# Where a whole group's outputs are scaled and where GpSimd's sums are called, in a mixture-of-experts tail on one core

## The chip, the core and the metric

The kernel runs on one core of a Trainium2 chip, in fp32. The metric is the device time of one execution in microseconds (us), given as the median of several runs. The profile is of one execution with the hardware profiler. Five engines run side by side, each with its own list of instructions in order: TensorE (PE, with its weight loads PEld), VectorE (DVE), ScalarE (ACT), GpSimd (POOL) and SyncE (SP, which here only issues DMAs). They wait for one another by semaphores.

## What is computed

One layer: a graph step (`adj @ h`), then a transformer block whose feed-forward part is a mixture of 8 experts, of which each token uses two. The change lies in the experts alone:

```python
flat = _rmsnorm(x, ln2_w).reshape(-1, Cx)
probs = jax.nn.softmax(flat @ router_w.T, axis=-1)
tp, ti = jax.lax.top_k(probs, TOPK)
tp = tp / (jnp.sum(tp, axis=-1, keepdims=True) + 1e-09)
weights = jnp.sum(tp[..., None] * jax.nn.one_hot(ti, NE, dtype=flat.dtype), axis=1)
out = jnp.zeros_like(flat)
for e in range(NE):
    hh = jax.nn.silu(flat @ w1[e].T) * (flat @ w3[e].T)
    out = out + weights[:, e:e + 1] * (hh @ w2[e].T)
return x + out.reshape(Bx, Tx, Cx)
```

There are 4096 tokens of 256 features; an expert has 682 hidden features.

## The kernel before

The kernel writes each token's row to the lists of its two experts in DRAM, and then works through groups of tokens of one expert: whole groups of 256 tokens (number below `NW`, 25) and small ones of 128 for what is left over. `TURNS` sets the order, and `k` is the place in it, from 0 to 41. Places 0 to 8 are whole groups. From 9 on whole and small groups alternate, except that places 15 and 16, 24 and 25, and 31 and 32 are two small groups in a row; 39, 40 and 41 are whole. So between 9 and 39 a whole group comes either behind one small group (k = 10, 12, 14, 19, 21, 23, 28, 30, 35, 37, 39) or behind two (k = 17, 26, 33).

The main loop (from L1984) does for each k: the hidden layer of group k (`hidden` or `hidden_seven`), then `combine(k - 1)`, the second layer of the group before with the weighting and the output, and then the loads of the weights and tokens of groups k + 4 and k + 5. TensorE so has the work of two groups between each other.

**Hidden layer in seven products.** Whole groups from k = 12 to 39 (`SPLIT13`) use `hidden_seven`: the matrix product in 2x2 blocks with seven block products instead of eight, in two parts, `one` (four chunks of 128 hidden features) and `two` (one chunk). Each part has three PSUM banks: hA, hD and hB. `begun` makes the first product in hA, which ScalarE copies to `s1`, the second in hD, which it copies to `s5`, and the third in hB. `second` adds a product to hA, copied by ScalarE to `u2`, and one to hD. `added_up` adds hB to `s1` and hD to `u2` on VectorE; between these it transposes token rows of coming groups (`turn`). `third` adds once more to hA. All these products are L1609, the copies L1615, the additions L1618. `multiplied` (L1653, L1654) makes the hidden values in SBUF, and `split` (L1704 to L1707) their four block sums on VectorE.

**The block sums of the first weights** are made by GpSimd in `sums13` (L1542 to L1545), four sums of 128x640 values. It is called at the end of an iteration and takes the next group of `SPLIT13` in turn, if that is at most five places ahead and fewer than two are waiting. Before the change it is called whenever `TURNS[k - 1]` is a whole group. Those of the second weights are made by VectorE in `sums2` (L1723 to L1726), right behind the hidden layer of the small group that comes before a whole one.

**combine.** For groups in `SEVEN` (whole, from k = 4 to 39) `seven_products` (L1747) makes seven products in two PSUM banks, ye_y and ye_ms; ScalarE copies one (L1754) and VectorE makes seven additions (L1755 to L1761). A small group has plain products (L1846) in bank ye_y. Both pools have one bank. `gates` makes the tokens' weights on VectorE: `pick` (L1505) and `gt` (L1510). ScalarE scales the output by `gt` (L1857), in two halves for a whole group and one for a small one. For each half GpSimd issues an indirect DMA that adds the rows to DRAM (L1868), behind a memset of `gap` (L1867).

**Order of the loads.** Behind the outputs of an iteration GpSimd sets a cell, `sent` (L2005); SyncE writes that cell to DRAM (L2006) and only then issues the loads that stand behind it in its queue: second weights `load2` (L1403), first weights `load13` (L1397), tokens `load_squares` (L1441) and rows `load_rows` (L1448).

The PSUM banks of the hidden layers are a pool of six (`e_h`), used in turn.

Of the kernel before, what the change touches and what calls it, by code (L numbers as in the profile page):

```python
# [45 lines left out]
NW = -((NE * (GR - 1) - 2 * N) // GR)  # L46
# [5 lines left out]
ALONE = 9  # L52
LAST = 3
RARE = 4
NM = NG - RARE
TURNS = list(range(ALONE)) + [
    g for _, g in sorted(
        ((g - first + 0.5) / (end - first), g)
        for first, end in ((ALONE, NW - LAST), (NW, NM)) for g in range(first, end)
    )  # L60
] + list(range(NW - LAST, NW)) + list(range(NM, NG))
# [5 lines left out]
def fast_kernel(  # L67
# [618 lines left out]
    with (  # L686
# [707 lines left out]
        def load13(k):  # L1394
            i = TURNS[k]
            expert_of[i] = entry(table[0:1, 1, i : i + 1], NE - 1)
            nc.sync.dma_start(  # L1397
                w13s[k % 5], w13[bass.ds(expert_of[i], 1)].rearrange("o p c w -> p (o c) w")
            )

        def load2(k):
            i = TURNS[k]
            nc.sync.dma_start(  # L1403
                w2s[k % 5],
                w2[bass.ds(expert_of.pop(i), 1)].rearrange("o p k c -> p (o k) c"),
            )
# [26 lines left out]
        def load_squares(k):  # L1433
            i = TURNS[k]
            n = halves(i)
            z = squares_room(k)[:, 0 : n * C].rearrange("p (m e) -> p m e", e=2 * Q)
            tokens = lists[bass.ds(place_of(i), n * P), 0:C].rearrange(
                "(m i) (g e) -> g i m e", i=Q, g=4
            )
            for g in range(4):  # L1440
                loaded(i, nc.sync.dma_start(z[g * Q : (g + 1) * Q], tokens[g]))  # L1441
# [45 lines left out]
        def turn(k):  # L1487
            n = halves(TURNS[k])
            turned = squares_room(k + 4)[:, 0 : n * C]
            nc.vector.transpose(turned, squares_room(k)[:, 0 : n * C])  # L1490
            turned_of[k] = turned.rearrange("p (m c i) -> p c m i", c=2, i=Q)
# [9 lines left out]
        def gates(k, r):  # L1501
            i = TURNS[k]
            n = halves(i)
            pick = ex.tile([P, n, NE], F32, tag="pick", name=f"pick_{i}")
            nc.vector.tensor_mul(  # L1505
                pick, r[:, 0:n, 1:KEPT],
                mine[:, i : i + 1, :].to_broadcast([P, n, NE]),
            )
            gt = ex.tile([P, n, 1], F32, tag="gt", name=f"gt_{i}", bufs=3)
            nc.vector.tensor_reduce(gt, pick, AX.X, ALU.add)  # L1510
            return gt
# [55 lines left out]
                )  # L1567
            sums13_of[k].update(m)

        def hidden_seven(k, step, behind):  # L1570

            i = TURNS[k]
            m, xT, w13_sb = sums13_of.pop(k), inputs_of.pop(i), w13s[k % 5]
# [43 lines left out]
            def added(dst, q, bank):  # L1617
                nc.vector.tensor_add(dst, dst, bank[:, 0 : len(q.chunks), :])  # L1618

            def begun(q):  # L1620
                product(q, q.A, "A11", "B11", True)
                copied(q.s1, q, q.A)
                product(q, q.D, "S1", "T1", True)
                copied(q.s5, q, q.D)
                product(q, q.B, "A12", "B21", True)

            def second(q):
                product(q, q.A, "S2", "T2")
                copied(q.u2, q, q.A)
                product(q, q.D, "S4", "B22")  # L1630

            def added_up(q, behind=()):
                behind = iter(behind)
                for j in behind:
                    turn(j)
                    break
                added(q.s1, q, q.B)
                for j in behind:
                    turn(j)
                added(q.u2, q, q.D)  # L1640

            def third(q):
                product(q, q.A, "S3", "T3")
# [13 lines left out]

            sums2(k)
            begun(one)
            second(one)  # L1660
            added_up(one, turns_in.pop(k, []))
            step()
# [155 lines left out]
        def combine(k):  # L1818
            i = TURNS[k]
            n = halves(i)  # L1820
            w2_sb = w2s[k % 5]
            hT = hidden_of.pop(i)
            r = rows.pop(i)
            gt = gates(k, r)
            if k < ALONE or k % 2:
                y = ax.tile([P, HALF, C], F32, tag="yT1", name=f"y_{i}")
            else:
                y = (
                    pt_all[:, 2 * (2 * W13 + W2) :] if k % 4
                    else wo_sb.rearrange("p j o -> p (j o)")[:, 0:512]  # L1830
                ).rearrange("p (h c) -> p h c", h=HALF)

            last = k >= NM - 2
            seven = k in SEVEN
            if seven:
                done = seven_products(k)
            else:
                ps = [
                    pool.tile([P, HALF, C], F32, tag=tag, name=f"ye_{i}_{tag}")
                    for pool, tag in ((p_ms, "ms"), (p_y, "y"))[0 if last else 1 :]  # L1840
                ]

            def products(h):
                cols = slice(h * P, (h + 1) * P)
                for q in range(NF + 1):
                    nc.tensor.matmul(  # L1846
                        ps[h if last else 0][:, h, :],
                        hT[:, q, cols], w2_sb[:, q, :], start=(q == 0), stop=(q == NF),
                    )

            for h in range(0 if last or seven else n):
                products(h)
            for h in range(n):
                if last:
                    products(h)
                if seven or n == 1:
                    nc.scalar.activation(  # L1857
                        y[:, h, :],
                        done[h].rearrange("p h o -> p (h o)") if seven else ps[0][:, h, :],
                        AF.Copy, scale=gt[:, h],  # L1860
                    )
                else:
                    nc.vector.tensor_scalar(
                        y[:, h, :], ps[h if last else 0][:, h, :], gt[:, h], None, op0=ALU.mult
                    )
                at = bass.IndirectOffsetOnAxis(ap=r[:, h, 0:1].bitcast(I32), axis=0)
                nc.gpsimd.memset(gap, 0.0)  # L1867
                put = nc.gpsimd.indirect_dma_start(  # L1868
                    out=(acc_dram if k < NM - LAST else out)[:, :],
                    out_offset=at,  # L1870
                    in_=y[:, h, :], in_offset=None, compute_op=ALU.add,
                )
                if h:
                    free(put, f"half {i}", "an expert has a token once")
                else:
                    join(put, f"half {i}")
                if i < NA:
                    free(put, "last x", "the tokens of the first groups are others")
                    join(put, "first sums")
# [92 lines left out]
        def step():  # L1972
            for f in next(rest, []):
                f()

        sent = ax.tile([1, 1], F32, name="sent", bufs=1)
        sent_dram = tc.dram_tile([1, 1], F32, name="sent_dram")
        load13(2)
# [5 lines left out]
        for k in range(NM):  # L1984
            if k == 3:
                sc_scope.close()
                p_h.append(ctx_h.enter_context(tc.tile_pool(name="e_h", bufs=6, space=PSUM)))
            if k == NM - 1:


                between = iter([lambda: None, lambda: combine(k - 1)])
            if k in SPLIT13:
                hidden_seven(k, step, k + 1)
            else:
                hidden(
                    k, step if k < NM - 1 else lambda: next(between)(),
                    k + 1 if k + 1 < NM else None,
                )
            step()
            if k + 1 in SPLIT13 and TURNS[k] >= NW:  # L2000
                sums2(k + 1)
            if 0 < k < NM - 1:
                combine(k - 1)
                if k + 4 < NM:
                    nc.gpsimd.memset(sent, 0.0)  # L2005
                    nc.sync.dma_start(sent_dram, sent)  # L2006
            if k + 4 < NM:
                load2(k + 4)
            if k + 5 < NM:
                load13(k + 5)  # L2010
            if k + 4 < NM:
                if k + 5 < NM:
                    load_squares(k + 5)
                load_rows(k + 4)
            if 0 < k < NM - 1:
                step()
                if k >= ALONE and TURNS[k - 1] < NW:
                    sums13(k)
            if k == NM - LAST:
                nc.sync.dma_start(out, acc_dram[0:N, :])  # L2020
        combine(NM - 1)
        ctx_h.close()
    kv_scope.close()
    return lists
# [739 lines left out]
```

## Time and profile before

| what | us |
|---|---|
| runs before (three), median | 1534.4 |
| lowest and highest of them | 1533.94, 1540.28 |
| the profiled execution | 1535.82 |
| its span in the profile | 1534.1 |

The span is from the first to the last recorded instruction of the core; the execution's time has 1.7 us around it. The page cuts the span into 40 equal slices, of 38.4 us each; a digit is the busy share of an engine in tenths, and PEclk is the clock that was granted to TensorE:

```profile
PE   9999999999999999999999999999999999998997
DVE  7764665755755677879879878785676767776772
ACT  2102012021021456665665655653222333333331
POOL 2102022121221331374554653452524545536342
PEclk9999999999999999999999999999999999999999
DMA  6344444543544000011011011059778897988765
```

The experts are the last third, from about slice 27. There TensorE is busy nearly all the time, GpSimd about half of it, and the DMA engines at 0.7 to 0.9. An instruction's line in the timeline has its start, its duration, engine and line, what it writes and reads, its shape, how many were merged, and in brackets how long the engine stood idle before it and what ended that.

### The profile page before, as it was taken

To read this page: it belongs to the slowest core of one execution; us is meant where nothing else is said; L and a number is where in the kernel's file an instruction comes from. 1 tells how busy PE (TensorE), PEld (TensorE's weight loads), DVE (VectorE), ACT (ScalarE), POOL (GpSimd) and SP (SyncE) were. 2 spreads that over 40 slices of the span, in tenths; PEclk is the share of its full clock that TensorE was granted. 3 is DMA by queue.
4 is the path that set the end of the run, shared out by engine and by line. 5 is a ranking of instruction groups with operands and counts; after the bars stand their busy time and mean duration, and the time that the engine had idled before them with its cause. 6 is when DMAs were issued, how large, how long until landed. Compare 5 with 4: busy or idle time off the path is not lost. (4 is left out here: it accounts for less than half of the span.)

```text
span 1534.1 us, 28641 instructions
## 1 busy us (share of the span) xinstructions
PE 1509.4 (98%) x10795; PEld 1113.2 (73%) x10795; DVE 1067.1 (70%) x2223; ACT 551.0 (36%) x991; POOL 559.2 (36%) x649
## 2 busy tenths in 40 slices
PE   9999999999999999999999999999999999998997
PEld 8888888888888543444444444358899999998996
DVE  7764665755755677879879878785676767776772
ACT  2102012021021456665665655653222333333331
POOL 2102022121221331374554653452524545536342
PEclk9999999999999999999999999999999999999999
DMA  6344444543544000011011011059778897988765
GB/s 240 131 134 151 156 141 147 167 153 121 178 141 151 4 1 30 15 58 33 26 57 37 29 37 36 22 156 325 211 208 222 261 269 219 269 246 239 225 150 136
DMA packets 105774, 212.19 MB, mean 138 GB/s; under 512 B 62394, under 2 KB 82106, under 8 KB 91994
## 3 DMA queue, kind: packets, MB, share of 16 engines
q1 hardware_dynamic: 92090, 192.00, 38.6%
q0 software_dynamic: 12720, 17.47, 6.3%
q8 instruction: 87, 1.43, 0.4%
q10 hardware_dynamic: 816, 0.79, 0.2%
q14 instruction: 61, 0.50, 0.1%
HBM read 184.48 MB, written 27.13 MB: 138 GB/s over the span
## 5 line engine op out<-in xcount | busy, mean ns | idle before, releaser
L785 PE MATMUL sc<-qT_all,kT 64*64 64x512 f32 (+3 forms) x2304 | 282.1, 557 | 0.5 <-ACT pt_all L793 0.3
L532 PE MATMUL acc<-a,g 128*128 128x256 f32 x1024 | 244.0, 379 | 0.0
L532 PEld LDWEIGHTS acc<-a,g 128*128 128x128 f32 x1024 | 193.5, 190 | 31.8 <-issue 6.7
L785 PEld LDWEIGHTS sc<-qT_all,kT 64*64 64x64 f32 x2304 | 91.2, 133 | 128.6 <-issue 109.2
L793 ACT ACTIVATE pt_all<-sc 128x1024 f32<-128x1024 f32 (+3 forms) x157 | 148.6, 954 | 96.9 <-PE sc L785 93.3
L532 PE MATMUL acc<-more_sums,g 128*128 128x256 f32 x512 | 126.3, 379 | 0.0
L1868 POOL DMA_INDIRECT acc_dram<-y,late x40 | 62.6, 1564 | 172.2 <-ACT y L1857 99.6
L813 DVE TENSOR_TENSOR late<-late,pt_all 128x1024 f32<-128x1024 f32 (+3 forms) x91 | 106.8, 1173 | 24.3 <-POOL pt_all L795 9.9
L433 ACT COPY qT_all<-tr 128x512 f32<-128x512 f32 x30 | 16.2, 588 | 258.7 <-PE tr L431 258.7
L532 PEld LDWEIGHTS acc<-more_sums,g 128*128 128x128 f32 x512 | 97.2, 190 | 13.2
L827 PE MATMUL y_first<-pt_all,vv 64*64 64x512 f32 (+3 forms) x448 | 106.6, 554 | 0.0
L625 POOL TENSOR_TENSOR rot<-rot,tables 128x512 f32<-128x512 f32 x21 | 33.6, 1601 | 198.6 <-ACT rot L621 158.4
L827 PE MATMUL y_second<-pt_all,vv 64*64 64x512 f32 (+3 forms) x436 | 104.2, 555 | 0.0
L1790 PE MATMUL h<-late,qT_all 128*128 128x256 f32 (+1 forms) x616 | 104.0, 327 | 0.1
L1790 PEld LDWEIGHTS h<-late,qT_all 128*128 128x128 f32 x616 | 93.5, 191 | 9.8 <-ACT late L1477 1.0
L1075 POOL DMA_INDIRECT lists<-row,slots x64 | 88.3, 1380 | 17.5 <-issue 15.0
L1797 DVE TENSOR_TENSOR late<-si,h 128x256 f32<-128x256 f32 (+2 forms) x87 | 39.4, 466 | 78.6 <-ACT si L1796 53.3
L827 PE MATMUL y_third<-pt_all,vv 64*64 64x512 f32 (+3 forms) x372 | 88.7, 555 | 0.0
L621 ACT ACTIVATE rot<-pq 32x512 f32<-32x512 f32 x84 | 49.4, 588 | 82.6 <-DVE qT_all L619 43.6
L813 DVE TENSOR_TENSOR sum_all<-sum_all,pt_all 128x1024 f32<-128x1024 f32 (+3 forms) x51 | 56.0, 1098 | 15.8 <-POOL pt_all L795 9.5
L793 ACT ACTIVATE late<-sc 128x1024 f32<-128x1024 f32 (+3 forms) x55 | 50.9, 927 | 41.4 <-PE sc L785 36.7
L532 PE MATMUL acc<-qT_all,g 128*128 128x256 f32 x256 | 65.7, 379 | 0.0
(493 smaller groups left out, 3301.4 us busy)
## 6 DMA issues: line engine op xcount, KB each, us to landing
a<-in_adj_dram SPq DMA_DIRECT2D x64, 1024.0 KB
qT_all<-in_w_dram SPq DMA_DIRECT2D x18, 1408.0 KB
pt_all<-in_w_dram SPq DMA_DIRECT2D x16, 1408.0 KB
res_all<-in_w_dram SPq DMA_DIRECT2D x17, 768.0 KB
pt_all<-in_w_dram SPq DMA_DIRECT2D x16, 768.0 KB
res_all<-in_w_dram SPq DMA_DIRECT2D x8, 1408.0 KB
qT_all<-in_w_dram SPq DMA_DIRECT2D x9, 768.0 KB
late<-lists SPq DMA_DIRECT2D x96, 64.0 KB
```

The lines of the kernel that those rows point to most:

```text
L433: nc.scalar.copy(dst[:, :, cols], tr.rearrange("p c t i -> p c (t i)"))
L532: nc.tensor.matmul(acc[bank][:, at, :], g[jb][:, right, k, :], m[left][:, k, :], start=(jb == 0 and k == 0 and at == 0), stop=(jb == NB - ...
L621: nc.scalar.activation(rot[n * Q : (n + 1) * Q, :], pj[(n ^ 1) * Q : ((n ^ 1) + 1) * Q, :], AF.Copy, scale=1.0 if n % 2 else -1.0,)
L625: nc.gpsimd.tensor_mul(rot, rot, tables[b][:, 1, :])
L785: nc.tensor.matmul(ps[k * HP : (k + 1) * HP, j, :w], kT[sb][hd, i * P + k * HP : i * P + (k + 1) * HP], qT[b][hd, p, off:], start=True, st ...
L793: nc.scalar.activation(pt[:, :, :w], ps[:, :, :w], AF.Exp, scale=HD ** -0.5)
L813: nc.vector.tensor_add(sums[b, p][:, :, off:], before[:, :, off:], pt[:, :, : 512 - off])
L827: nc.tensor.matmul(accs[b, p][k][hd, off:], vv[sb][some, i, hd], pt[some, j, : 512 - off], start=(s == order_of(b)[0]), stop=(s == order_o ...
L1075: put = nc.gpsimd.indirect_dma_start(out=lists[:, :], out_offset=bass.IndirectOffsetOnAxis(ap=chosen[b][:, k, t, :], axis=0), in_=flats[b] ...
L1790: nc.tensor.matmul(ps[m % 2][:, m // 2 - q, :], w13_sb[:, c, m * P : (m + 1) * P], xT[:, c, :], start=(c == 0), stop=(c == 1),)
L1797: nc.vector.tensor_mul(hT[:, q : q + both, :], si[:, 0:both, :], ps[1][:, 0:both, :])
L1868: put = nc.gpsimd.indirect_dma_start(out=(acc_dram if k < NM - LAST else out)[:, :], out_offset=at, in_=y[:, h, :], in_offset=None, comput ...
```

## The change

Four things change. (1) `combine` becomes a generator that stops behind its products and, for a whole group, its seven additions; `gates`, the scaling and the output DMAs come when it is resumed, so `gates` stands behind the additions for every group. (2) In iterations with a small group between two whole ones (`k + 1 in SPLIT13`, `k - 1 in SEVEN`; k = 11, 13, 18, 20, 22, 27, 29, 34, 36, 38) this rest, with the `sent` cell, the loads and `sums13`, becomes the function `ended`, which `hidden_seven` of the next group calls as `pending`, behind `begun(one)`, that is behind the copies to `s1` and `s5`. In all other iterations `ended` runs at once. (3) `sums13` is called in the iteration of a small group that has a whole group behind it, where it was called in the iteration behind a whole group. For one small group between whole ones that is the same iteration; for two in a row it is the second one instead of the first. (4) In `added_up` the first `turn` comes behind the first addition and the second behind the second, each one step later than before.

```diff
-        def hidden_seven(k, step, behind):
+        def hidden_seven(k, step, behind, pending=None):
...
             def added_up(q, behind=()):
-                behind = iter(behind)
-                for j in behind:
-                    turn(j)
-                    break
                 added(q.s1, q, q.B)
-                for j in behind:
+                for j in behind[0:1]:
                     turn(j)
                 added(q.u2, q, q.D)
+                for j in behind[1:]:
+                    turn(j)
...
             begun(one)
+            if pending:
+                pending()
             second(one)
...
             r = rows.pop(i)
-            gt = gates(k, r)
...
             for h in range(0 if last or seven else n):
                 products(h)
+            yield
+            gt = gates(k, r)
...
+        def whole(outputs):
+            for _ in outputs:
+                pass
+
+        pending = []
...
-                between = iter([lambda: None, lambda: combine(k - 1)])
+                between = iter([lambda: None, lambda: whole(combine(k - 1))])
             if k in SPLIT13:
-                hidden_seven(k, step, k + 1)
+                hidden_seven(k, step, k + 1, pending.pop() if pending else None)
...
-            if 0 < k < NM - 1:
-                combine(k - 1)
-                if k + 4 < NM:
+            outputs = combine(k - 1) if 0 < k < NM - 1 else iter([None, None])
+            next(outputs)
+
+            def ended(k=k, outputs=outputs):
+                next(outputs, None)
+                if 0 < k < NM - 1 and k + 4 < NM:
                     nc.gpsimd.memset(sent, 0.0)
                     nc.sync.dma_start(sent_dram, sent)
-            if k + 4 < NM:
-                load2(k + 4)
-            if k + 5 < NM:
-                load13(k + 5)
-            if k + 4 < NM:
+                if k + 4 < NM:
+                    load2(k + 4)
                 if k + 5 < NM:
-                    load_squares(k + 5)
-                load_rows(k + 4)
-            if 0 < k < NM - 1:
-                step()
-                if k >= ALONE and TURNS[k - 1] < NW:
-                    sums13(k)
+                    load13(k + 5)
+                if k + 4 < NM:
+                    if k + 5 < NM:
+                        load_squares(k + 5)
+                    load_rows(k + 4)
+                if 0 < k < NM - 1:
+                    step()
+                    if k >= ALONE and TURNS[k] >= NW and TURNS[k + 1] < NW:
+                        sums13(k)
+
+            if k + 1 in SPLIT13 and k - 1 in SEVEN and TURNS[k] >= NW:
+                pending.append(ended)
+            else:
+                ended()
...
-        combine(NM - 1)
+        whole(combine(NM - 1))
```

## The prediction

> **What bounds the kernel now.** I read the totals, then TensorE's row in the list of waits, then busy time by stretch of the expert stage (from about 1034 us on), then the timeline round each gap. TensorE is busy for 1509.4 of 1534.1 us; between 1190 and 1490 us it stands still in one place only, which the list of waits names:
>
> ```profile
> PE 1509.4 (98%) x10795; PEld 1113.2 (73%) x10795; DVE 1067.1 (70%) x2223; ACT 551.0 (36%) x991; POOL 559.2 (36%) x649
> ...
> PE hA L1609 <- issue: 12.5, 10, 4.5
> ...
> 1350.00:1390.00 40.00, 39.10 (x325) 38.27 (x325) 28.19 (x73) 16.31 (x42) 20.89 (x22) 1.00 0.87 244
> 1390.00:1430.00 40.00, 35.50 (x267) 34.46 (x266) 27.10 (x57) 11.98 (x33) 16.75 (x19) 0.91 0.79 234
> ```
>
> Ten gaps, 12.5 us, the longest 4.5, all ahead of an hA product: hA is written again by `second(one)` after ScalarE has copied its first result. Stretches without a long gap have 0.5 to 2 us idle; that from 1390 us has 4.5 and a clock of 0.91. No TensorE wait on a load is listed. The gap ahead of group k=39:
>
> ```profile
> 1478.59 1.06 PE L1609 MATMUL hA<-late,pt_all 128*128 128x128 f32 x8
> ...
> 1480.47 1.03 ACT L1857 ACTIVATE y<-vv,gt 128x256 f32<-128x256 f32 x2 [3.42 <-DVE vv L1759]
> ...
> 1481.40 0.56 ACT L1615 COPY wqkv_sb<-hA 128x512 f32<-128x512 f32 x1
> ...
> 1482.07 1.13 PE L1609 MATMUL hA<-kT,sum_all 128*128 128x128 f32 x8 [0.64 <-issue]
> ```
>
> The copy of hA could start at 1479.7; it stands behind the two scalings of the last whole group's output, which wait for VectorE's sums. The worst gap, k=33, whose two predecessors are both small:
>
> ```profile
> 1407.02 1.79 POOL L1542 TENSOR_TENSOR sum_all<-qT_all 128x640 f32<-128x640 f32 x1 [1.21 <-DMA qT_all<-in_w_dram]
> ...
> 1407.45 1.77 DVE L1724 TENSOR_TENSOR pt_all<-pt_all 128x384 f32<-128x384 f32 x1
> ...
> 1412.77 1.49 DVE L1505 TENSOR_TENSOR pick<-late,mine 128x8 f32<-128x8 f32 x1
> ...
> 1414.54 0.47 ACT L1857 ACTIVATE y<-ye_y,gt 128x256 f32<-128x256 f32 x1 [8.06 <-issue]
> ...
> 1415.59 2.05 PE L1609 MATMUL hA<-kT,res_all 128*128 128x128 f32 x8 [4.50 <-issue]
> ```
>
> While GpSimd makes its four sums (L1542 to L1545, 1407 to 1414 us) each of VectorE's sums of two SBUF operands takes 1.77 to 1.89 us instead of 0.56, and a 128x8 one 1.49 instead of 0.17. The scaling is late, the copy behind it, and hA. The lock also shows in a whole group itself:
>
> ```profile
> 1221.01 1.77 DVE L1653 TENSOR_TENSOR late<-qT_all,hy 128x512 f32<-128x512 f32 x1
> ...
> 1487.67 0.69 DVE L1653 TENSOR_TENSOR late<-wqkv_sb,hy 128x512 f32<-128x512 f32 x1
> ```
>
> The first (k=14) runs beside GpSimd's sums, the second (k=39) has none beside it.
>
> **What the Trainium skill says.** "SBUF — State Buffer", "SBUF: two separate sides": a VectorE operation with two SBUF inputs and a GpSimd operation that reads SBUF lock each other out for a whole instruction. The trace agrees (1.77 against 0.56 us above), and VectorE's additions from PSUM (L1618, 0.69 us) aren't slowed. "TensorE: Matmul & The Clock Gate", "What's actually happening": after an idle window of about 3.4 us the clock halves. It does after the 4.50 us gap (2.05 us for eight products, else 1.06 to 1.13) and after none under 2 us. Same page, "Architectural detail": ScalarE and VectorE take instructions strictly in order; the copy behind the scalings agrees. "PSUM — Partial Sum Buffer", "PSUM bank collisions": banks have to be guarded by semaphores, so bank ye_y isn't written before its reader is done. No wait of that kind is in the trace yet; I count on one below.
>
> **What goes.** The gaps of weight loads sum to 14.1 us (same list, PEld row; matmul ends are modelled, so PE's 12.5 is 0.16 a gap less). The cold clock after the 4.5 us gap: hA to hD takes 1.84 us against 0.97, hD on to the next hA 1.70 against 0.89, three pairs 1.19 against 0.66: 2.2 us. Together 16.3 us. By place: three whole groups behind two small ones (k=17, 26, 33) hold 0.91, 2.12, 4.67 and the 2.2 of clock, 9.9 us; seven of the ten behind one small group (k=12, 14, 21, 23, 30, 37, 39) hold 1.58, 0.79, 0.70, 0.80, 1.06, 0.72, 0.80, 6.4 us.
>
> **Behind two small groups (sums called one group later).** No GpSimd sums lie beside L1723 to L1726 any more. But the gates of the whole group's output (pick and gt, 0.38 us) move behind its seven additions, and the scaling then waits for the last of these instead of the fifth (0.5 us): 0.87 us on ScalarE and VectorE. For k=33: sums2 from 1407.73 (1406.86 before) to 1409.98, gates to 1410.33, y 1410.43, copy 1410.80 to 1411.37, hA 1411.42 against 1410.91 without a gap. Three times 0.5 = 1.5 us stay, at full clock; 8.4 go.
>
> **Behind one small group (deferred).** Time zero is the whole group's first hA; from its second hA on I subtract the gap, since TensorE and what hangs on it come forward by it. The copies run at +1.15 and +2.0, so second hA is free at +2.67: the gap itself goes. The scalings are now third and fourth on ScalarE, at +2.5 at the earliest (before, less the gap: k=35 +0.84, k=37 and 39 about +1.1), the copy to u2 behind them. GpSimd's first sum really starts 4.28 us after the first scaling (k=35: 1436.90 to 1441.2: two DMA issues, the `sent` memset of 0.6 us): +6.8 instead of +5.1 to +6.3. Loads follow the same memset, 1 to 1.5 us later against TensorE; at four groups ahead (over 30 us) that costs nothing, unless DMA (0.84 busy from 1190 to 1490 us) backs up.
>
> What late sums cost is in the trace. Start of the first sum, and of the small group's scaling y behind `split` (L1704 to L1707) and its gates: k=35 +5.1 and +14.4; k=37 +5.3 and +14.6; k=23 +5.6 and +14.8; k=30 +5.7 and +14.9; k=14 +6.3 and +15.6; without sums (k=39) +13.3. About 1 us per us. Laying out the lock by hand for +6.8: L1653 (one) slips through at +8.3, L1653 (two) waits until +10.2, L1704 until +11.8, L1705 until +13.6; L1707 ends at +15.4, y starts at +15.75.
>
> Two things then wait for y. The next seven products begin at +16.26 (k=37: 1473.90) and write ye_y, which y reads for 0.47 us: free if y starts by +15.65, so 0.1 us lost. And sums2 for the next whole group end at its zero plus (y - 14.6) us (k=35 to 37: 14.4 gives -0.2), here +1.05 after the loss. From there its additions (2.1), gates (0.38), two scalings and u2's copy (1.6) end near +5.1, when the third hA is due: 0.1 lost. Its sums start at +7.8; now L1653 (one), (two), L1704 and L1705 all wait, y is at +16.7, and 1.04 us are lost at ye_y, after which the next group stands at +1.05 again. So the chain through VectorE, ScalarE and GpSimd takes over from the second such group in a row on.
>
> Sum: first in a row after k=19, 28, 35: 0.2 each; after k=12, which starts late (sums2 end at +0.65): 0.8; second and later, after k=14, 21, 23, 30, 37: 1.04, plus 0.1 twice: 5.4. Together 6.8 stay where 6.4 were: nothing gained there.
>
> **Edits with one answer.** The order of `turn` and `added` only reorders 0.44 to 0.70 us on VectorE, with over 1 us before their readers. Elsewhere gates move without a VectorE operation between, or (whole groups in a row, k=4 to 10) 0.87 us later under 14 us of TensorE work a group.
>
> **Sum.** 16.3 - 1.5 - 6.8 = 8.0 us. The profiled execution took 1535.8 us, 1.7 over its span and 1.4 over the median; 1534.4 - 8.0 = 1526.4.
>
> **Unknowns.** The wait at ye_y: zero to 1.4 us a place (six places); I take 1.04. Who gets the lock when both stand ready: one blocked operation more or less, 1.2 us a cycle; I alternate, as at 1407 to 1414 us. The residue behind two small groups: 0 to 0.7. These give 4 to 11 us of gain.
>
> **Rivals.**
> - The gaps go and nothing follows: the whole 16.3, less 1.5: 1519.6 us. For it: ScalarE is busy only 36%, and the small group's y had 1.2 us to spare. Against it: the row of y above.
> - No net change: the deferred chain costs 1.5 us a cycle over nine cycles with sums (13.5) and 1.5 stay: 1533.
> - Slower: GpSimd's sums come down on the whole of `split`. If the first starts after about +9.5, all of L1704 to L1707 wait 1.2 us each, y is at +18.2, and 2.6 us are lost in each of nine cycles: 23.4 + 1.5 - 16.3 = 8.6 us, 1543. It decides from 1.65 us a cycle on. For it: nothing pulls a late chain back but the pairs of small groups. Against it: in my layout the loss at ye_y holds the sums at +7.8.
>
> **How the numbers follow.** Likeliest case 0.45 (1523 to 1530), nothing follows 0.28, no net change 0.12, slower 0.15. A measurement of this kernel tells about 0.5% (7.7 us, so below 1526.7) from no change. Faster: half of the first and the second, 0.51; same 0.34; slower 0.15. The range of 1518.5 to 1533.5 holds the first three.
>
> **What would show it.** Second hA without a gap behind one small group; at k=33 a gap near 0.5 us and no clock under 1; L1704 and L1705 above 1 us where one was; new idle time of TensorE ahead of ye_y (L1747). I am wrong if ye_y never waits (then 1520), or if hA's gaps stay.

## The result, and the profile after

| | median us | lowest, highest | runs |
|---|---|---|---|
| before, on the same chip | 1533.9 | 1528.6, 1540.3 | 11 |
| after | 1528.4 | 1527.0, 1531.4 | 11 |

The ratio is 0.9969, with a 95% interval of 0.9955 to 0.9984: 4.8 us less by the ratio (2.5 to 6.9), 5.5 us by the medians. The forecast was 1526.4. The profiled executions are 1535.82 and 1529.01 us, the spans 1534.1 and 1527.3. The after runs lie within 4.4 us of each other, the before runs within 11.7; that difference is part of the story.

The totals of the kernel after, and TensorE's row in its list of waits in the expert stage (waiting operation, what it waited for; us in total, times, longest):

```profile
PE 1507.6 (99%) x10795; PEld 1110.9 (73%) x10795; DVE 1079.4 (71%) x2223; ACT 550.3 (36%) x991; POOL 561.2 (37%) x649
```

```profile
PE ye_y L1747 <- ACT y L1858: 3.5, 5, 1.1
PE ye_y L1747 <- ACT wo_sb L1858: 1.6, 2, 0.8
PE ye_y L1747 <- ACT pt_all L1858: 1.4, 1, 1.4
```

The line `hA <- issue` with its 12.5 us is gone. In its place stand three that before did not have at all: the first of a whole group's seven products (L1747) waits at bank ye_y until ScalarE has scaled the small group before it, whose output lies in that bank (the releaser's name is only that of the buffer which y happens to be in). VectorE is busy 12 us longer than before, though it has the same 2223 instructions: more of them wait while they hold the engine. Line numbers differ a little between the kernels: the scaling L1857 of before is L1858 here, the indirect DMA L1868 is L1869, and L1653 is L1651.

By stretch, the same two as before (columns: us, busy PE, PEld, DVE, ACT, POOL with counts, clock, DMA share, GB/s):

```profile
1350.00:1390.00 40.00, 39.74 (x326) 38.72 (x326) 32.08 (x77) 16.34 (x42) 20.24 (x22) 1.00 0.84 230
1390.00:1430.00 40.00, 38.95 (x322) 37.97 (x321) 28.94 (x71) 12.92 (x36) 18.26 (x21) 1.00 0.89 266
```

From 1390 us on the clock is 1.00 instead of 0.91 and 322 matmul records lie where 267 lay. Now the places. This is the timeline at k=39, behind one small group:

```profile
1472.19 1.06 PE L1609 MATMUL hA<-late,pt_all 128*128 128x128 f32 x8
...
1473.29 0.59 ACT L1615 COPY wqkv_sb<-hA 128x512 f32<-128x512 f32 x1 [2.64 <-PE hA L1609]
...
1474.87 1.06 PE L1609 MATMUL hA<-kT,sum_all 128*128 128x128 f32 x8
...
1475.66 0.91 ACT L1858 ACTIVATE y<-vv,gt 128x256 f32<-128x256 f32 x2 [0.89 <-DVE gt L1510]
```

The copy follows the first hA by 1.1 us and waits for nothing else, the second hA has no idle time in brackets, and the scalings come behind the copies. At k=33, behind two small groups:

```profile
1407.80 0.56 DVE L1724 TENSOR_TENSOR pt_all<-pt_all 128x384 f32<-128x384 f32 x1
...
1409.33 0.16 DVE L1505 TENSOR_TENSOR pick<-late,mine 128x8 f32<-128x8 f32 x1
...
1409.77 0.47 ACT L1858 ACTIVATE y<-ye_y,gt 128x256 f32<-128x256 f32 x1 [3.46 <-PE hA L1609]
...
1410.82 1.13 PE L1609 MATMUL hA<-kT,res_all 128*128 128x128 f32 x8
...
1413.20 2.12 POOL L1542 TENSOR_TENSOR sum_all<-qT_all 128x640 f32<-128x640 f32 x1
```

L1724 takes 0.56 us where it took 1.77, L1505 0.16 where it took 1.49, y is 4.8 us earlier, hA has no gap and runs at full clock (1.13 us, before 2.05). GpSimd's first sum starts at 1413.20, when VectorE's are over.

And where the new wait comes from, k=37 and the small group behind it (its first hA began at 1450.26):

```profile
1453.72 0.91 ACT L1858 ACTIVATE y<-vv,gt 128x256 f32<-128x256 f32 x2 [0.89 <-DVE gt L1510]
...
1457.39 2.14 POOL L1542 TENSOR_TENSOR sum_all<-pt_all 128x640 f32<-128x640 f32 x1
...
1458.47 1.61 DVE L1651 TENSOR_TENSOR late<-qT_all,hy 128x512 f32<-128x512 f32 x1
...
1462.32 1.20 DVE L1704 TENSOR_TENSOR kT<-late 128x384 f32<-128x384 f32 x1
...
1463.55 1.78 DVE L1705 TENSOR_TENSOR kT<-kT,late 128x384 f32<-128x384 f32 x1
1465.37 0.56 DVE L1706 TENSOR_TENSOR kT<-late,kT 128x384 f32<-128x384 f32 x1
...
1466.87 0.47 ACT L1858 ACTIVATE wo_sb<-ye_y,gt 128x256 f32<-128x256 f32 x1 [7.66 <-PE h L1790]
...
1467.40 1.60 PE L1747 MATMUL ye_y<-res_all,late 128*128 128x128 f32 x12 [0.79 <-ACT wo_sb L1858]
```

Read it from the top, counting from that first hA: the scalings are late, so the outputs are late, so GpSimd's sums are late (L1542 is recorded from +7.1, but its end and its usual 1.54 us say that it really ran from +7.7), so L1651, L1704 and L1705 wait on the lock, so y is at +16.6, and TensorE stands at ye_y.

By the weight loads' rows (PEld, as in the prediction) the ten gaps ahead of hA (14.1 us) and the cold clock (2.2) are gone, and ten waits at ye_y have come, 8.5 us in all. By the place k of the iteration in which TensorE waits they are 0.43 at position 11, then 0.99, 1.31, 0.33, 0.98, 1.60, 0.45, 1.24, 0.22 and 0.98 at positions 13, 15, 20, 22, 24, 29, 31, 36 and 38. That is 7.8 us gained by gaps; the span is 6.8 us shorter. At the end of the stage GpSimd's outputs wait for transfers to land, which takes 0.4 of it; the other 0.6 is spread over matmul records whose ends are modelled, and I cannot place it.

### The profile page after: what moved, and what is told of

Same layout as the page of the kernel before. It is cut to its first block, busy times and chain, and to the rows that moved or that the text cites. A ratio compares the mean times of both kernels' runs of the same rounds, so it can differ in the third digit from the quotient of the medians.

```text
span 1527.3 us, 28639 instructions
## 1 busy us (share of the span) xinstructions
PE 1507.6 (99%) x10795; PEld 1110.9 (73%) x10795; DVE 1079.4 (71%) x2223; ACT 550.3 (36%) x991; POOL 561.2 (37%) x649
## 4 chain that ended last, share of the span: by engine, by line
PE 96%; DMA 1%; DVE 1%; issue 1%; ACT 1%; POOL 0%; SPq 0%; POOLq 0%; ACTq 0%; DVEq 0%
PE acc L532 25%; PE sc L785 15%; PE h L1790 13%; PE y_first L827 5%; PE y_second L827 5%; PE y_third L827 4%; PE ye_y L1845 4%; PE hA L1609 4%; PE ye_y L1747 4%; PE ye_ms L1747 3%; PE pq L612 2%; PE hD L1609 2%; PE pf L503 2%; PE ph L193 2%; PE po L913 1%; PE hB L1609 1%
## 5 line engine op out<-in xcount | busy, mean ns | idle before, releaser
L1869 POOL DMA_INDIRECT acc_dram<-y,late x40 | 62.5, 1564 | 178.2 <-ACT y L1858 94.5
```

Source lines behind the costliest of these rows:

```text
L1869: put = nc.gpsimd.indirect_dma_start(out=(acc_dram if k < NM - LAST else out)[:, :], out_offset=at, in_=y[:, h, :], in_offset=None, comput ...
```

## The experiments

The theory after this comparison: the gain comes from part (3) alone (sums in front of a whole group), and the deferral, part (2), only carries the wait from hA to ye_y, because what is late is a chain (GpSimd's sums, VectorE's sums behind them, the scaling behind these) and not a place in ScalarE's order. The rival: both parts earn their share by place, the deferral the gaps behind one small group. Each set of runs had its own runs of before beside it; before's medians were 1533.9, 1537.8, 1537.7 and 1539.5 us on four occasions, so kernels of different sets are compared by their ratios.

### Before, once more

No edit; is the profile of before typical?

> The kernel before, unchanged, for a second trace of it. The trace on record has a gap of 4.67 us ahead of k=33 and 2.2 us of half clock behind it, from a GpSimd sum that waited 1.21 us for a load and then met VectorE's L1724 to L1726. Theory: that gap hangs on when the load lands, so it is of another size here (0.5 to 5 us, at k=17, 26 and 33 alike), while the gaps behind one small group (k=12, 14, 21, 23, 30, 37, 39) are within 0.2 us of 1.58, 0.79, 0.70, 0.80, 1.06, 0.72 and 0.80. Rival: all gaps repeat within 0.2 us, and the trace on record is typical.

1537.06 us. The gaps behind one small group came back to within 0.02 us; those behind two did so only at k=26: they are 2.12, 2.12 and 3.46 us at k=17, 26 and 33, where the profile of before has 0.91, 2.12 and 4.67. Products at k=17 and 26, timeline of this run:

```profile
1246.06 1.64 PE L1609 MATMUL hA<-kT,sum_all 128*128 128x128 f32 x8 [1.96 <-issue]
1247.50 1.91 PE L1609 MATMUL hD<-late,sum_all 128*128 128x128 f32 x8
...
1342.53 1.13 PE L1609 MATMUL hA<-kT,sum_all 128*128 128x128 f32 x8 [1.96 <-issue]
```

The first of them is followed by a cold clock (1.91 us for eight products), the second, with the same gap, is not. So these places of before vary from execution to execution, two of the three in length, and in the clock behind them. There GpSimd's first sum is called a group earlier and waits for its load (1.2 to 3.0 us in the two profiles), which sets where the four sums fall on VectorE's. The sum of the three gaps, though, is 7.7 us in both profiles.

The clock tells more of before's wide range of times. In the 30 runs of before beside the next three kernels the time follows the mean clock that the run was granted: 1532.2 us at 0.998, a median of 1536.9 at 0.996 and of 1541.4 at 0.994, 1547.7 at 0.992, about 2.4 us for each thousandth (correlation -0.96). One stretch of 3.41 us at half clock takes 0.0011 off the mean. By an estimate from these figures 1.5 of the 2.4 us are the slower clock itself (a thousandth of 1535 us); the rest may be longer gaps. Of the eleven runs after the change ten have 0.998, and the slowest, 1531.4 us, has 0.996.

### Part (3) alone, on before

```diff
-                if k >= ALONE and TURNS[k - 1] < NW:
+                if k >= ALONE and TURNS[k] >= NW and TURNS[k + 1] < NW:
```

> The kernel before with part (3) alone: GpSimd's sums are called in front of a whole group instead of behind one. Theory: the gaps at k=17, 26 and 33 go (7.7 us and 2.2 of clock in the trace on record), the rest keep their hA gaps of 0.7 to 1.6 us, and k=19, 28 and 35 stay without one; 3 to 8 us faster than before, that is all of what the whole change gains or more. Rival, that the deferral is what gains: no more than 2 us faster.

1529.65 us, ratio 0.9947 (0.9926 to 0.9968), and a profiled span of 1527.3 us, that of the whole change. TensorE's list of waits:

```profile
PE hA L1609 <- issue: 7.7, 9, 1.4
```

The gaps at k=17, 26 and 33 are gone, the cold clock with them (all nine runs have 0.998 or 0.999). The whole gain is here. One detail of the expectation failed: k=19 and 28, the second whole groups, now have gaps of 1.20 and 1.31 us that were not there. The sums were moved one group later, beside k=17 and k=26, and that whole group's chain, it seems, hands its delay on. Weight-load gaps total 9.2 us, 4.9 less than in the profiles of before; the other 3 of the 8 us that the ratio gives may be the clock.

### The deferral without part (3)

The changed kernel with the old condition for `sums13`, the edit above in reverse: parts (1), (2) and (4) together.

> The changed kernel with the old condition for GpSimd's sums: the deferral and the two reorderings without part (3). Theory: the gaps behind one small group move from hA to ye_y (0.2 to 1.3 us each) without getting less, the gaps at k=17, 26 and 33 stay at hA; within 3 us of the kernel before. Rival, that the deferral gains: 4 us or more faster.

1539.34 us, ratio 1.0009 (0.9995 to 1.0023): nothing. Its list of waits:

```profile
PE hA L1609 <- issue: 6.3, 2, 3.8
PE ye_y L1747 <- ACT y L1858: 2.9, 4, 1.1
PE ye_y L1747 <- ACT wo_sb L1858: 1.6, 2, 0.8
PE ye_y L1747 <- ACT pt_all L1858: 0.8, 1, 0.8
```

The gaps ahead of hA behind one small group have become waits at ye_y; the two of hA that remain are k=17 (2.62 us) and k=33 (3.98), both followed by a cold clock. At k=26, where the expectation had a third, there is none: there GpSimd's first sum waited 3.43 us for its load and came behind VectorE's four. The rival falls.

### Without GpSimd's sums

If the lock between GpSimd's sums and VectorE's is the cause of what is left, leaving out the four sums must leave TensorE without a gap, whichever order ScalarE has. In both kernels the four sums of the weight blocks are left out, so the products of whole groups read blocks that nobody has made; all else stays.

```diff
-            nc.gpsimd.tensor_add(m["S1"], m["A21"], m["A22"])
-            nc.gpsimd.tensor_sub(m["S2"], m["S1"], m["A11"])
-            nc.gpsimd.tensor_sub(m["S4"], m["A12"], m["S2"])
-            nc.gpsimd.tensor_sub(m["S3"], m["A11"], m["A21"])
```

On the changed kernel:

> The changed kernel without GpSimd's four block sums of the first weights (the products read what lies in their rooms). Theory, that the lock between GpSimd's sums and VectorE is what is left: the ten waits at ye_y (8.5 us in the trace of the changed kernel) vanish, L1704 to L1707 take 0.56 us each, 7 to 9 us faster than the changed kernel, about 1520 us. Rival, that the chain is long by itself (order of gates, ScalarE): the waits at ye_y stay at 0.5 us or more each, less than 3 us faster.

On before:

> The kernel before without GpSimd's four block sums of the first weights. Theory: with no lock VectorE's chain is 1.3 us ahead of TensorE (as in k=35 of the trace of before, which had no gap), so the hA gaps vanish although the scalings stand ahead of the copies; 1518 to 1521 us, as the changed kernel without the sums. Rival, that the order on ScalarE makes the gaps behind one small group: these (0.7 us each, 6 us in all) stay, 1525 us or more.

1519.49 us, ratio 0.9884 (0.9852 to 0.9916), and 1520.85 us, 0.9894 (0.9866 to 0.9923). Busy time from 1100 to 1500 us, first before, then after, then after without the sums, then before without them:

```profile
1100.00:1500.00 400.00, 387.51 (x2941) 372.33 (x2940) 282.64 (x694) 136.90 (x350) 177.25 (x196) 0.99 0.81 229
```

```profile
1100.00:1500.00 400.00, 393.35 (x2995) 377.41 (x2994) 297.73 (x705) 137.85 (x355) 178.98 (x196) 1.00 0.82 234
```

```profile
1100.00:1500.00 400.00, 400.00 (x3039) 384.88 (x3038) 265.72 (x710) 139.58 (x357) 96.51 (x148) 1.00 0.84 237
```

```profile
1100.00:1500.00 400.00, 398.82 (x3034) 383.95 (x3033) 268.76 (x724) 141.19 (x359) 93.37 (x144) 1.00 0.85 241
```

TensorE is busy for all of the 400 us; VectorE spends 32 us less, with slightly more instructions in the stretch. In before only the gap at k=12 is left (1.4 us), though its scalings still stand ahead of the copies: the order on ScalarE costs next to nothing in these two kernels. The runs take away GpSimd's work and its queue time together; that it is the lock is read from the lines above, where VectorE's operations lengthen only beside a sum.

### The sums in front of the outputs

So the sums have to lie elsewhere: beside VectorE's additions from PSUM, which the lock doesn't touch (in before L1618 takes 0.69 us beside a sum and away from one). In iterations with a small group between two whole ones the gates are made first, GpSimd copies one column of them (so that it starts no earlier), and its sums go ahead of the outputs; the call of `sums13` at the end of these iterations falls away.

```diff
+            if early:
+                gt = gates(k, r)
+                nc.gpsimd.tensor_copy(gap, gt[:, 0])
+                sums13(k + 1)
...
-            gt = gates(k, r)
+            if not early:
+                gt = gates(k, r)
```

With the deferral:

> The changed kernel with GpSimd's sums ahead of the whole group's outputs where there is one small group between: gates in front of the seven additions, GpSimd copies a column of gt first and then makes the sums, the outputs follow. Theory: the sums run from about 0.5 to 7 us behind the whole group's first hA, where VectorE has only operations with a PSUM operand, L1704 to L1707 take 0.56 us, the ye_y waits go; 1519 to 1523 us. Rival: outputs, `sent` and loads come 3 to 4 us later, and loads or GpSimd's queue become the bound; 1527 us or more, with waits of GpSimd or TensorE on loads.

Without it, on before with part (3):

> The kernel before with GpSimd's sums in front of a whole group and, where there is one small group between, ahead of the outputs and behind the gates, without the deferral. Theory: the same time as with the deferral, 1519 to 1523 us, and no hA gap of more than 0.3 us, as nothing is late any more. Rival: without the deferral hA gaps of 0.5 us or more stay, 3 us or more slower than with it.

1540.16 us, 1.0018 (1.0007 to 1.003), and 1541.53 us, 1.0029 (1.0015 to 1.0043): both slower than before, by 0.2 and 0.3%. Where the sums ran at once (behind k=12) L1704 to L1707 took 0.56 us each, y came at +13.28, and nothing waited, as the theory has it. Elsewhere this happened (timeline, with the deferral; the first line is of the sums called at k=13, the others lie at k=33):

```profile
1220.51 1.53 POOL L1542 TENSOR_TENSOR sum_all<-res_all 128x640 f32<-128x640 f32 x1 [9.97 <-DMA res_all<-in_w_dram]
...
1424.66 0.71 DVE L1490 STREAM_TRANSPOSE late<-late 128x512 f32<-128x512 f32 x1 [4.09 <-DMA late<-lists]
...
1426.00 2.20 PE L1609 MATMUL hA<-kT,pt_all 128*128 128x128 f32 x10 [3.12 <-DVE hy L1618]
```

`sums13` sums for the next whole group not yet summed, and that can be four places ahead, whose load is called for only in the iteration before. GpSimd's first sum waited 30 us for loads in five places, 27.6 of them in the three (k=13, 22 and 29) where it was four places ahead. Behind it in its queue stood the outputs, and behind these the loads: at k=33 VectorE stood 4.1 us for token rows, and TensorE behind VectorE. The expectation's rival named it.

### The sums in front only where the load is old

The sums go first only where the group that they are for is at most three places ahead.

```diff
+            alternate = k + 1 in SPLIT13 and k - 1 in SEVEN and TURNS[k] >= NW
+            first = alternate and unsummed and unsummed[0] - k < 4
+            outputs = combine(k - 1, first) if 0 < k < NM - 1 else iter([None, None])
```

With the deferral, and without it (on before with part (3)):

> As the changed kernel with sums ahead of the outputs, but only where the group whose sums are made is at most three places ahead (k=11, 18, 20, 27, 34, 36); where it is four ahead (k=13, 22, 29) the outputs go first as in the changed kernel. Theory: GpSimd no longer stands on a load that was only just issued (9 us each in three places when all sums went first), the six places have L1704 to L1707 at 0.56 us; ye_y waits are left at k=15, 24 and 31 (about 1 us each) and 1521 to 1525 us is reached. Rival, that late outputs and loads cost by themselves: 1528 us or more.

> The same on the kernel before, without the deferral and with part (3). Theory: 1521 to 1526 us, within 2 us of the one with the deferral, with hA gaps only where the sums still come last. Rival: 4 us or more slower than with the deferral.

With the changed kernel again in the same set:

> The changed kernel, on the same chip as these two, for a comparison with them. Expected at 0.994 to 0.998 of the kernel before, like part (3) alone (0.9947), and 3 to 7 us slower than the version with three places' lead.

| | median us | lowest, highest | ratio to before |
|---|---|---|---|
| sums first, deferral | 1524.99 | 1524.14, 1525.84 | 0.9908 (0.9883 to 0.9932) |
| sums first, no deferral | 1526.06 | 1524.36, 1526.8 | 0.9912 (0.9887 to 0.9937) |
| the change | 1529.08 | 1528.62, 1529.52 | 0.9934 (0.9909 to 0.9959) |

The change itself came out just below the 0.994 that was expected as its least. Both variants lie below every run of the change, and far below before. In the six places where the sums go first L1704 to L1707 take 0.56 us each. TensorE's list of waits, sums first with the deferral:

```profile
PE ye_y L1747 <- ACT y L1863: 2.3, 3, 1.5
PE ye_y L1747 <- ACT pt_all L1863: 1.4, 1, 1.4
```

Four waits at ye_y are left (4.4 us by the weight loads), at positions 11, 15, 24 and 31; the change has 8.2 in this set, and the 3.8 us between them are most of the 4.1 between the medians. The two variants differ by 1.1 us with overlapping ranges: on top of sums that are on time the deferral may bring a microsecond, or nothing. Where the variant without it loses is not where its expectation had it: its four hA gaps (4.9 us by the weight loads, at k=12, 19, 28 and 35) lie in places where the sums go first, so there the order on ScalarE does cost something.

## Why the prediction was right in place, and long in size

**The hA gaps go (16.3 us): held.** No hA gap is left, and k=33 runs at full clock. Of the rivals, "nothing follows" falls with the waits at ye_y, and "slower" because GpSimd's first sum at k=37 stayed at +7.7, against the +7.8 predicted and the +9.5 from which it would have decided. "No net change", 1533, lies above every run of after.

**The residue behind two small groups (1.5 us): it was nothing.** The prediction had the gates' move behind the additions delay y by 0.87 us through sums2 at 1407.73 to 1410.33. They began at 1407.20, only 0.34 us later than before (0.5 counted from the group's first hA, which itself came 0.16 earlier), as ScalarE's silu operations ahead of them (L1796) ran without the 0.74 us of idle time that lay between two of them before. So y came at 1409.77, 0.66 us earlier than predicted, which was inside the slack of the copy: no gap at hA.

**The waits at ye_y (6.8 us): right mechanism, 1.7 too few.** At k=37 the layout by hand gave y at +16.7 and a wait of 1.04; it was +16.6 and 0.98. At positions 13, 22 and 38 it was 0.98 or 0.99. The first in a row (20, 29, 36) had 0.33, 0.45 and 0.22 where 0.1 to 0.2 was expected, and positions 15, 24 and 31 had 1.31, 1.60 and 1.24 instead of 1.04, so a chain that is late twice does not always stand at a fixed delay, as I had assumed. In the second profile of the change (last set) positions 24 and 31 had 0.98 and 1.00 and position 29 had 0.98, so these sizes differ from execution to execution. And position 11 had 0.43 us, where I had put the gates' move at nothing under 14 us of TensorE work, in "edits with one answer". That failed in a way the step didn't look at. The timeline of after:

```profile
1173.15 2.12 POOL L1542 TENSOR_TENSOR sum_all<-res_all 128x640 f32<-128x640 f32 x1
...
1178.89 1.54 DVE L1704 TENSOR_TENSOR kT<-late 128x384 f32<-128x384 f32 x1
...
1185.22 1.60 PE L1747 MATMUL ye_y<-qT_all,late 128*128 128x128 f32 x12 [0.24 <-ACT y L1858]
```

The later gates let the output go 0.89 us later (1172.11 against 1171.22), behind it on GpSimd start the sums, the last of them ends at 1180.0 instead of 1179.1 us, and L1704, 0.56 us alone, takes 1.54 us instead of 0.73. The cover was TensorE's; the cost came through GpSimd's queue and the lock. All five profiles with the gates' move and the sums have this wait (0.42 to 0.44 us), and none of the others has it.

The prediction also says that no wait of TensorE on a bank's reader is in the trace of before. The ten gaps ahead of hA are such waits: hA is written again once ScalarE has copied it. The step that counts on ye_y doesn't rest on this.

**The sum (8.0 us): close in the trace, partly by luck, and too long against the median.** By gaps the gain was 7.8: the residue's 1.5 and the waits' 1.7 happened to cancel. Against its own time the forecast for the profiled execution was 1535.8 - 8.0 = 1527.8; it took 1529.0, 1.2 more: 0.2 of gaps and the 1.0 of the stage's end and matmul records above. The other part is the base. I took the gaps of one execution off the median of the runs, and that execution was 1.9 us over the median of all eleven, while the profiled execution after was only 0.6 over its own. So the forecast seems to have counted as gain what the median run of before did not lose. Which part of the 9.9 us at k=17, 26 and 33 that is, no trace shows: both profiles of before have 7.7 us of gaps there. The clock of the 30 runs suggests the cold stretches behind them, at 2.4 us for a thousandth, but this stays an inference.

The prediction named 0.5% as the bound of what can be told from no change, and the forecast was just past it. The result, 0.31% (0.16 to 0.45), is within it; beside the before of the last set, 1539.5 us, the same kernel is 0.66% faster (0.41 to 0.91). Between these two sets the median of the change moved by 0.7 us and that of before by 5.6.

**What of it each part earned.** The prediction said that nothing is gained behind one small group and that 8.4 us go behind two. The runs of the parts agree: 0.9947 for part (3), 1.0009 for the other three together.

## What to carry to other kernels

When an operation in an in-order queue waits for a late input, moving it behind others takes the wait off these and leaves the input as late as it was; ask first what makes it late, and what stands behind it next. Here it was four GpSimd sums beside VectorE's operations on two SBUF operands, and the remedy was to put them beside work that reads PSUM, but only where their own inputs have long landed, since everything behind them in the queue waits with them. And a gap whose length depends on when a transfer lands needs a second profile before it is counted, with the clock behind it.

## What was not expected of the hardware

The prediction relied on the Trainium skill's "TensorE: Matmul & The Clock Gate", "What's actually happening", for a half clock after about 3.4 us idle. Here the clock also fell after idle times of about 2 us: in the second profile of before at k=17, shown above, and in the kernel with the sums first, whose timeline has

```profile
1261.69 2.21 PE L1747 MATMUL ye_y<-res_all,late 128*128 128x128 f32 x12 [2.01 <-ACT wo_sb L1863]
...
1359.49 1.60 PE L1747 MATMUL ye_y<-res_all,late 128*128 128x128 f32 x12 [2.08 <-ACT y L1863]
```

The same twelve products take 2.21 us after 2.01 us of idle time, and 1.60 after 2.08. So the length of the gap alone doesn't decide at this size. What does can be worked out from the clock in the traces. Between 1100 and 1500 us each stretch at half clock lasts 3.41 us (one lasts 6.83, twice that), and where an execution has two, they begin 170.67 us (second profile of before), 170.67 (deferral alone) or 163.84 (sums first, deferral) apart: 50, 50 and 48 times 3.413. So they lie on a grid of 3.413 us. Laid on that grid, the gaps come apart. First the two of the second profile of before, then the two of the kernel with the sums first (columns as above, with the clock third from the end):

```profile
1243.10:1246.51 3.41, 1.45 (x14) 1.29 (x13) 2.75 (x5) 1.44 (x3) 3.33 (x3) 1.00 1.06 439
1246.52:1249.93 3.41, 3.41 (x19) 3.41 (x18) 1.20 (x3) 0.64 (x2) 3.08 (x5) 0.50 0.45 122
1338.68:1342.09 3.41, 1.89 (x17) 1.70 (x16) 3.12 (x4) 0.61 (x2) 3.25 (x3) 1.00 1.04 391
1342.09:1345.50 3.41, 2.97 (x26) 3.00 (x27) 2.00 (x3) 1.90 (x5) 3.26 (x5) 1.00 0.72 230
```

```profile
1259.10:1262.51 3.41, 1.40 (x13) 1.21 (x12) 1.88 (x5) 1.34 (x4) 0.74 (x3) 1.00 1.07 325
1262.52:1265.92 3.40, 3.40 (x18) 3.40 (x18) 2.97 (x10) 1.08 (x4) 1.00 (x2) 0.50 0.66 74
1354.68:1358.09 3.41, 2.73 (x25) 2.54 (x23) 3.31 (x4) 0.00 (x0) 2.37 (x3) 1.00 0.81 271
1358.09:1361.50 3.41, 2.01 (x18) 2.01 (x19) 1.69 (x6) 2.24 (x7) 1.59 (x2) 1.00 0.97 272
```

A gap that lies whole in one cell of the grid leaves PE idle for 1.96 or 2.01 of its 3.41 us, and the next cell has half clock. One that a border of the grid cuts into 1.52 and 0.44 us, or into 0.68 and 1.40, leaves the clock at 1.00. From 1100 to 1500 us of all twelve profiles (the grid laid from the half clock at the end, where there is none before) every cell at half clock follows one with at least 1.96 us of idle time, and none follows a cell with 1.70 or less. The border between the two isn't known better: at the very end of one execution a cell with 1.97 us idle is followed by full clock. For the price of a gap it matters: at k=33 the cold clock added 2.2 us.

And the lock, which "SBUF — State Buffer", "SBUF: two separate sides", describes as exclusive for a whole instruction, let the two engines alternate: L1651 above began at 1458.47, beside a GpSimd sum recorded until 1459.53, and ended at 1460.08, its usual 0.69 us after 1459.39, 0.14 us before that sum's recorded end (GpSimd's recorded times are rough). L1704 and L1705 behind it waited in the same way for one sum each. So a VectorE operation between two sums cost its own time plus what was left of one sum, not of the whole row of four.
